# Two-layer graph attention on one core: the loads and projections ahead of the pipeline in another order, and the second layer's last eight tiles in a loop of their own

## The chip, the cores and the metric

The kernel runs on one core of one Trainium2 chip. The metric is the device time of one launch in microseconds (us); lower is better. All times below are us unless marked ns.

## The reference, cut to what matters

Sixteen graphs of 1024 nodes with 256 features each go through two layers. All arithmetic is float32; `adj` is int32 with about 3% ones.

```
# layer 0: masked 8-head attention (HD = 32), pre-norm, residual
h = relu(layernorm(x))
Q, K, V = h Wq' + bq, h Wk' + bk, h Wv' + bv
x = x + softmax(where(adj == 0, -inf, Q K' / sqrt(32))) V  Wo' + bo
# layer 1: one head, edge scores by kind of edge, pre-norm, residual
h = relu(layernorm(x))
e_k = leaky_relu((h * a_k) h', 0.2)            for k = 0..3
x = x + softmax(where(adj == k + 1, e_k, -9e15)) h
```

With the inputs at hand only kind 1 occurs. The kernel computes layer 1 for that kind and checks at the very end, in a few small instructions on `kinds_seen`, whether another kind was present; if so a slow branch is taken, which never happens here.

## The kernel before

A graph has eight tiles of 128 rows, so there are 128 tiles. Everything is laid out by hand in one `tc.manual_schedule()` block: the order in which the Python code calls the methods is the order of the instructions on each engine's queue, and each engine works its queue strictly in that order. The DMAs are issued from queues too: SP's (`nc.sync`), ACT's (`nc.scalar`) and POOL's (`nc.gpsimd`). Each DMA that SP or ACT issues takes one of eight semaphores in turn, so it also waits until the DMA that had that semaphore before it has landed.

**Classes.** `Piece` normalises rows of `x`, turns them and projects them to keys, queries and values. `piece.load` reads `x`; `stats` runs `bn_stats` and `bn_aggr` on DVE and then `norm_of`, 18 tiny POOL instructions for 1/sqrt(variance); `normed` is the scaled ReLU on ACT; `turn` transposes on PE and copies on ACT (`hT`) and DVE (`hTm`); `project(which, oc)` multiplies on PE (which = 0 keys, 1 queries; oc one of two halves of the features); `high` (ACT) and `split` (DVE) cut the result into two halves that add up to it exactly, and `split` issues the DMAs that write them to DRAM (`kd` for keys, `qd` for queries), each twice, once from SP and once from ACT when the piece has four tiles; `values` makes V. `load_key(b, h)` reads one head's keys back from `kd`, `Attend.load_queries` reads one tile's queries from `qd` (`qt`).

`Attend` is layer 0 for one tile: `scores(h)` on PE, `softmax_max(h)` on DVE (L435), `softmax_exp(h)` on ACT (L443), then the probabilities are transposed, for half the heads by PE and ACT, for the other half by a DVE 32x32 block transpose (`blocks_of`, L364) and four DMAs that put the blocks in place (`placed`, L369); `combine` multiplies with V, and later steps project, add the residual, write `x1d` and normalise for layer 1 (`turn_normed`, `turned_normed` write the tile's columns of `h1T`).

`Edges` is layer 1 for one tile: `prepare` (POOL, `ha`), `score(0)`, `score(1)` (PE, L565, into the PSUM tile `sides[1]`), `softmax_max` and `leak` (DVE, L579, L587), `softmax_exp` (ACT, L591), `turn_blocks` (DVE, L364), `place_blocks` (four SP DMAs, L369), `gather(0)`, `gather(1)` (PE, L609), `load_nodes` (POOL DMA), `store` (DVE, L618, and an SP DMA). Its buffers `sel`, `ha`, `x1b`, `pT1` exist once each.

**Prologue.** Graph 0 cannot be projected inside the loop, so it is done ahead of it in two `Piece`s of four tiles each (`first`). Then come one tile of graph 1 (`piece_was`) and the load and statistics of the next (`piece_next`). In program order: the small bias loads and the four weights are loaded and the weights are transposed; the three pieces are loaded, then normalised one after the other; adjacency tile 0 is flagged and masked, adjacency tile 1 and `piece_next` are loaded from POOL's queue, `piece_next.stats()`; then both first pieces are turned, projected (for each piece keys, then queries), and their values made; then SP loads the queries of tile 0 and the eight heads' keys.

**Loop.** `for s in range(B * NT + LAG + 1)`, that is s = 0..137. At step s the body runs attention for tile s, the tail of attention for tile s-1, layer 1 for tile s-9 (`edge`, LAG = 9) and its gather for tile s-10 (`edge_was`), and the projections of the piece for tile s+9. From s = 129 on only layer 1 is left: the last eight tiles, all of graph 15, which go through the same loop body. There the body is, in order: `score(0)`, (once) the turn of the last layer-0 tile, `turn_blocks` and `place_blocks` of the tile before, `score(1)`, `load_nodes` of the tile before, `softmax_max`, `leak`, `prepare` of the next tile, `gather(0)`, `gather(1)` and `store` of the tile before, `softmax_exp`.

Of the kernel before, what the change touches and what calls it, by code (L numbers as in the profile page):

```python
# [8 lines left out]
F32 = mybir.dt.float32  # L9
# [8 lines left out]
P = 128  # L18
HEADS = 8
# [23 lines left out]
def gnn_kernel(  # L43
# [18 lines left out]
    nc = tc.nc  # L62
# [40 lines left out]
    a_t = const.tile([P, NC, N_KINDS], F32, name="a_t")  # L103
    with nc.allow_non_contiguous_dma(reason="a few hundred elements, once"):
        nc.sync.dma_start(out=bq_t, in_=bq.rearrange("(c p) -> p c", p=P))
        nc.sync.dma_start(out=bk_t, in_=bk.rearrange("(c p) -> p c", p=P))
        for k, a in enumerate((a_0, a_1, a_2, a_3)):
            nc.sync.dma_start(out=a_t[:, :, k], in_=a.rearrange("(c p) o -> p (c o)", p=P))
    bv_t = const.tile([P, D], F32, name="bv_t")
    bo_t = const.tile([P, D], F32, name="bo_t")  # L110
    for i in range(2):
        nc.sync.dma_start(
            out=bv_t[:, i * P : (i + 1) * P].rearrange("p (r d) -> p r d", r=2),
            in_=bv.rearrange("(r i d) -> i r d", i=2, r=2)[i].partition_broadcast(P),
        )
    nc.sync.dma_start(out=bo_t, in_=bo.partition_broadcast(P))

    def transposed_weight(w, name):

        rows = work.tile([P, NC, D], F32, tag="p", name=f"{name}_rows", bufs=4)  # L120
        nc.sync.dma_start(out=rows, in_=w.rearrange("(c p) f -> p c f", p=P))
        wt = const.tile([P, NC, D], F32, name=name)
        tr = ps_tr.tile([P, 4, P], F32, tag="tr", name=f"{name}_tr")
        for fc in range(NC):
            for oc in range(NC):
                nc.tensor.transpose(tr[:, fc * NC + oc, :], rows[:, oc, fc * P : (fc + 1) * P], ident)
        if name == "wvT":
            for fc in range(NC):
                nc.vector.tensor_copy(
                    wt[:, fc].rearrange("p (i r d) -> p r i d", i=2, r=2),  # L130
                    tr[:, fc * NC : (fc + 1) * NC].rearrange("p r (i d) -> p r i d", i=2),
                )
        else:
            nc.vector.tensor_copy(wt.rearrange("p c f -> p (c f)"), tr.rearrange("p c f -> p (c f)"))
        return wt

    wqT = transposed_weight(wq, "wqT")
    wkT = transposed_weight(wk, "wkT")
    wvT = transposed_weight(wv, "wvT")
    woT = transposed_weight(wo, "woT")  # L140


    def norm_of(mv):
# [4 lines left out]
        def place(name, dtype=F32):  # L148
            return small.tile([P, 4], dtype, tag=name, name=name)[:, :n]

# [19 lines left out]

    def stats_place(n):
        return small.tile([P, 4, nc.vector.BN_AGGR_DIM], F32, tag="mv", name="mv")[:, :n, :]

# [5 lines left out]

    qds, kds, vs, keysets = {}, {}, {}, {}  # L180

    class Piece:
# [66 lines left out]
        def project(self, which, oc):  # L249
            wT, bias = ((wkT, bk_t), (wqT, bq_t))[which]  # L250
            b, w = self.b, self.n * P
# [67 lines left out]
        def values(self):  # L319
            b = self.b  # L320
            if b not in vs:
                vs[b] = graph.tile([P, NT, D], F32, tag="v", name=f"v_{b}")
            for t in range(self.n):
                ps = (late, early, brief)[t % 3]
                self.vproj = ps
                for i, hT in enumerate((self.hTm, self.hT)):
                    for fc in range(NC):
                        nc.tensor.matmul(
                            ps[:, i * P : (i + 1) * P],
                            lhsT=hT[:, fc, t * P : (t + 1) * P],  # L330
                            rhs=wvT[:, fc, i * P : (i + 1) * P],
                            start=(fc == 0),
                            stop=(fc == NC - 1),
                        )
                if self.n > 1:
                    self.biased(t)
# [41 lines left out]
    class Attend:  # L378
# [111 lines left out]
        def output(self):  # L490
            self.y = late
            for g in range(NC):
                nc.tensor.matmul(
                    self.y, lhsT=self.oT[:, g, :], rhs=woT[:, g, :], start=(g == 0), stop=(g == NC - 1)
                )
# [51 lines left out]
    class Edges:  # L547
        def __init__(self, b, t):
            self.b, self.t = b, t
            self.rows = slice(t * P, (t + 1) * P)  # L550

        def prepare(self):
            self.ha = work.tile([P, NC, P], F32, tag="ha", bufs=1)
            for c in range(NC):
# [6 lines left out]
        def score(self, nh):  # L561
            cols = slice(nh * HALF, (nh + 1) * HALF)
            self.e = sides[1]
            for c in range(NC):
# [11 lines left out]
        def softmax_max(self):  # L576
            self.sel = work.tile([P, N], F32, tag="sel", bufs=1)
            top = small.tile([P, 1], F32, tag="top")
# [16 lines left out]
        def load_nodes(self):  # L595
            self.x1 = work.tile([P, D], F32, tag="x1b", bufs=1)
            nc.gpsimd.dma_start(out=self.x1, in_=x1ds[self.b][self.rows, :])
# [4 lines left out]
        def place_blocks(self):  # L602
            self.pT = placed(self.blocks, ptp.tile([P, N], F32, tag="pT1", name="pT1", bufs=1))

# [86 lines left out]
    def edges_of(s):  # L691
        s -= LAG
        return Edges(*divmod(s, NT)) if 0 <= s < B * NT else None

# [4 lines left out]
    with tc.manual_schedule():  # L699
        first = [Piece(0, 0, 4), Piece(0, 4, 4)]  # L700
        piece_was = Piece(1, 0)
        for piece in (*first, piece_was):
            piece.load(nc.sync)
        for piece in (*first, piece_was):
            piece.stats()
            piece.normed()
        now, piece_next = attend_of(0), piece_of(0)
        nxt = attend_of(1)
        now.load()
        now.flag()  # L710
        now.mask()
        nxt.load()
        piece_next.load()
        piece_next.stats()
        for piece in first:
            piece.turn()
        for piece in first:
            for which in range(2):
                for oc in range(NC):
                    piece.project(which, oc)  # L720
                    piece.high()
                    piece.split()
        for piece in first:
            piece.values()
        piece, edge, edge_was = piece_next, None, None
        now.load_queries()
        for h in range(HEADS):
            load_key(0, h)
        piece_was.turn()
# [5 lines left out]
        gone = was = None  # L735
        for s in range(B * NT + LAG + 1):
            b, t = divmod(s, NT)
# [142 lines left out]


        seen = small.tile([P, B], F32, tag="seen", bufs=1)
        nc.vector.tensor_reduce(seen, kinds_seen.rearrange("p (b t) -> p b t", t=NT), AX.X, ALU.max)
# [48 lines left out]
```

## Time and profile before

| | |
|---|---|
| median of 3 runs | 3300.01 (3297.72 to 3308.03) |
| the profiled execution: its time, its span | 3310.77, 3309.0 |
| busy, share of the span | PE 93%, DVE 85%, ACT 74%, POOL 52% |
| mean granted TensorE clock | 0.979 |
| first softmax instruction (DVE L435) starts | 80.04 |
| last tile's store (DVE L618) starts | 3298.66 |
| layer 1 alone (s = 129 to 137) | from about 3206 to 3299 |

The profile is one execution, and its times count from the start of its span; its own time lies 1.8 over its span, and 10.8 over the median of the runs. A timeline row gives the start, the duration, the engine, the line, the instruction, out<-in, the count, and in brackets the idle time before and what ended it. "DMA share" in a table of windows is the mean busy share of the core's 16 DMA engines.

### The profile page before, as it was taken

To read this page: it belongs to the slowest core of one execution; us is meant where nothing else is said; L and a number is where in the kernel's file an instruction comes from. 1 tells how busy PE (TensorE), PEld (TensorE's weight loads), DVE (VectorE), ACT (ScalarE), POOL (GpSimd) and SP (SyncE) were. 2 spreads that over 40 slices of the span, in tenths; PEclk is the share of its full clock that TensorE was granted. 3 is DMA by queue.
4 is the path that set the end of the run, shared out by engine and by line. 5 is a ranking of instruction groups with operands and counts; after the bars stand their busy time and mean duration, and the time that the engine had idled before them with its cause. 6 is when DMAs were issued, how large, how long until landed. Compare 5 with 4: busy or idle time off the path is not lost. (4 is left out here: it accounts for less than half of the span.)

```text
span 3309.0 us, 98026 instructions
## 1 busy us (share of the span) xinstructions
PE 3080.0 (93%) x36018; PEld 2239.0 (68%) x36018; DVE 2802.7 (85%) x5111; ACT 2458.4 (74%) x4829; POOL 1735.3 (52%) x3902
## 2 busy tenths in 40 slices
PE   4888999999999999999999999999999999998997
PEld 2666767777676767767677677776766676676653
DVE  2887989989898989989899888989988899898963
ACT  2887878778787877878778777878777788787750
POOL 2555555555555555555555555555555555555531
PEclk9898999999999999999999999999999999999999
DMA  5777787877878787787878878787787877877642
GB/s 187 219 232 227 235 262 221 269 225 235 264 221 267 225 254 241 223 261 228 255 229 240 245 229 253 228 261 237 229 257 218 250 235 231 252 231 242 197 136 70
DMA packets 747063, 762.93 MB, mean 231 GB/s; under 512 B 71280, under 2 KB 692080, under 8 KB 746576
## 3 DMA queue, kind: packets, MB, share of 16 engines
q1 hardware_dynamic: 678288, 542.21, 55.3%
q0 software_dynamic: 65088, 210.16, 19.9%
q8 instruction: 290, 4.75, 0.6%
q10 hardware_dynamic: 3200, 4.19, 0.3%
q14 instruction: 197, 1.61, 0.1%
HBM read 252.98 MB, written 167.77 MB: 127 GB/s over the span
## 5 line engine op out<-in xcount | busy, mean ns | idle before, releaser
L435 DVE CUSTOM_DVE_ANT_0 p<-s,neg 128x1024 f32<-128x1024 f32 x1024 | 1233.6, 1205 | 150.6 <-issue 120.5
L443 ACT ACTIVATE p<-p,nmx 128x1024 f32<-128x1024 f32 x1024 | 1178.4, 1151 | 221.2 <-DVE nmx L435 219.7
L423 PE MATMUL s<-k,qt 128*128 128x512 f32 x2048 | 797.3, 471 | 21.8 <-DVE nmx L435 9.8
L478 PE MATMUL acc<-pT,v 128*32 128x128 f32 x16384 | 561.0, 283 | 112.3 <-DMA pT<-blocks 110.7
L544 ACT COPY pT<-trp 128x512 f32<-128x512 f32 x1024 | 543.8, 582 | 162.6 <-PE trp L543 151.9
L403 POOL TENSOR_SCALAR neg<-adj 128x1024 bf16<-128x1024 int32 x128 | 467.0, 3648 | 359.3 <-ACT neg L415 358.9
L364 DVE STREAM_TRANSPOSE blocks<-p 128x1024 f32<-128x1024 f32 x512 | 632.2, 1235 | 0.1
L478 PEld LDWEIGHTS acc<-pT,v 128*32 128x32 f32 x16384 | 472.1, 114 | 196.8 <-issue 119.4
L543 PE MATMUL trp<-ident,p 128*128 128x128 f32 x4096 | 534.2, 274 | 0.2 <-ACT pT L544 0.2
L543 PEld LDWEIGHTS trp<-ident,p 128*128 128x128 f32 x4096 | 481.0, 141 | 74.0 <-ACT pT L544 3.6
L609 PE MATMUL acc<-h,pT 128*32 128x256 f32 x8192 | 509.9, 383 | 12.5 <-DMA pT<-blocks 11.8
L565 PE MATMUL s<-h1T,ha 128*128 128x512 f32 x1024 | 482.8, 595 | 0.5 <-ACT h1T L522 0.5
L423 PEld LDWEIGHTS s<-k,qt 128*128 128x128 f32 x2048 | 331.1, 192 | 155.0 <-issue 107.7
L609 PEld LDWEIGHTS acc<-h,pT 128*32 128x32 f32 x8192 | 246.6, 110 | 228.5 <-issue 78.0
L462 POOL COPY wide<-rec 128x256 f32<-128x256 f32 x128 | 51.0, 398 | 573.3 <-DVE rec L460 573.3
L309 POOL DMA_DIRECT2D kd<-halves x240 | 169.6, 707 | 238.6 <-DVE halves L282 230.6
L579 DVE CUSTOM_DVE_ANT_0 sel<-s,neg 128x1024 f32<-128x1024 f32 x128 | 156.8, 1225 | 146.2 <-PE s L565 146.2
L565 PEld LDWEIGHTS s<-h1T,ha 128*128 128x128 f32 x1024 | 175.3, 191 | 130.0 <-issue 128.6
L591 ACT ACTIVATE sel<-sel,nmx 128x1024 f32<-128x1024 f32 x128 | 145.5, 1137 | 70.8 <-DVE rec L616 64.9
L443 ACT ACTIVATION_READ_ACCUMULATOR p<-p,nmx 128x1 f32 x1024 | 193.7, 189 | 0.0
L472 ACT COPY recT<-acc 128x256 f32<-128x256 f32 x128 | 47.8, 373 | 176.7 <-PE acc L468 176.7
L261 PEld LDWEIGHTS acc<-hT,wkT 128*128 128x128 f32 x960 | 119.5, 195 | 76.1 <-issue 46.9
(106 smaller groups left out, 4008.3 us busy)
## 6 DMA issues: line engine op xcount, KB each, us to landing
pT<-blocks SPq DMA_DIRECT2D x2560, 128.0 KB, 3.5
qt<-qd SPq DMA_DIRECT2D x128, 512.0 KB, 5.5
adj<-in_adj POOLq DMA_DIRECT2D x127, 512.0 KB, 4.8
qd<-halves SPq DMA_DIRECT2D x240, 256.0 KB, 3.2
k<-kd POOLq DMA_DIRECT2D x120, 512.0 KB, 7.0
kd<-halves SPq DMA_DIRECT2D x240, 128.0 KB, 3.8
kd<-halves POOLq DMA_DIRECT2D x240, 128.0 KB, 3.6
xb<-in_x POOLq DMA_DIRECT2D x128, 128.0 KB, 3.0
```

Source lines behind the costliest of these rows:

```text
L309: queue.dma_start(out=kds[self.b][oc, :, :, twice, self.cols], in_=halves.rearrange("p (w n) -> p w n", w=2),)
L364: nc.vector.transpose(blocks.rearrange("p b j q -> p j b q"), p)
L403: nc.gpsimd.tensor_scalar(self.neg, self.adj, 0.0, MASKED, ALU.is_equal, ALU.mult)
L423: nc.tensor.matmul(self.ps[:, cols], lhsT=self.qt[:, h, :], rhs=keysets[self.b][h][:, cols], start=True, stop=True,)
L435: nc.vector.tensor_tensor_reduce(out=p, in0=sides[h in (3, 5, 7)], in1=self.neg, scale=-SCALE, scalar=FLOOR, op0=ALU.add, op1=ALU.min, acc ...
L443: nc.scalar.activation(p, p, AF.Exp, bias=nmx, scale=-1.0, accum_out=self.sums[:, h : h + 1])
L478: nc.tensor.matmul(sums_place[r * HD : (r + 1) * HD, g * P : (g + 1) * P], lhsT=vs[self.b][:, j, place_of(h) : place_of(h) + HD], rhs=self ...
L543: nc.tensor.transpose(tr[:, j, :], p[:, jj * P : (jj + 1) * P], ident)
L544: copy(pT[:, half * 4 : half * 4 + 4, :], tr)
L565: nc.tensor.matmul(self.e[:, cols], lhsT=self.ha[:, c, :], rhs=h1Ts[self.b][:, c, cols], start=(c == 0), stop=(c == NC - 1),)
L579: nc.vector.tensor_tensor_reduce(out=self.sel, in0=self.e, in1=masks[self.b, self.t], scale=-1.0, scalar=3e38, op0=ALU.add, op1=ALU.min, a ...
L609: nc.tensor.matmul(sums_place[a * HD : (a + 1) * HD, :], lhsT=self.pT[:, j, a], rhs=h1s[self.b][:, j, :], start=(j == 0), stop=(j == NT - 1),)
```

## The change

The prologue is laid out anew. SP first loads `x` of graph 0, then the four weights (`load_weights`), then `piece_was`, adjacency tile 0, the biases (`load_biases`) and `piece_next`, which moves from POOL's queue to SP's. The statistics of the two first pieces go into one place, and one `norm_of` with eight columns serves both. The weights are transposed after that. All key projections of both pieces come ahead of all query projections, and the eight `load_key` are issued between the two. `load_queries` comes behind the query projections; flag, mask and the load of adjacency tile 1 come after them too, and `piece_next.stats()` after the values. The values of a four-tile piece use the two rotating `ps_tr` tiles of PSUM.

The loop ends after s = 128. The last eight tiles of layer 1 run in a loop of their own: tile k's scores are put ahead of the gather of tile k-2, the scores alternate between `sides[0]` and `sides[1]`, `turn_blocks` of tile k-1 stands ahead of `store` of tile k-3, and the buffers for `sel`, `pT1`, and for odd tiles `ha` and `x1b`, come from pools with free slots. The diff, cut where lines only moved into a function:

```diff
+    def load_biases():
...
+    weight_rows = {}
+
+    def load_weights():
+        for w, name in ((wk, "wkT"), (wq, "wqT"), (wv, "wvT"), (wo, "woT")):
+            weight_rows[name] = work.tile([P, NC, D], F32, tag="p", name=f"{name}_rows", bufs=4)
+            nc.sync.dma_start(out=weight_rows[name], in_=w.rearrange("(c p) f -> p c f", p=P))
...
         def place(name, dtype=F32):
-            return small.tile([P, 4], dtype, tag=name, name=name)[:, :n]
+            if n <= 4:
+                return small.tile([P, 4], dtype, tag=name, name=name)[:, :n]
+            places.append(name)
+            return many[:, len(places) * n - n : len(places) * n].bitcast(dtype)
...
-                ps = (late, early, brief)[t % 3]
+                ps = late if self.n == 1 else ps_tr.tile([P, D], F32, tag="tr", name="vproj")
...
     class Edges:
-        def __init__(self, b, t):
+        def __init__(self, b, t, last=False):
...
+            self.side = sides[t % 2 if last else 1]
+            self.tags = {"sel": ("p", 4), "pT1": ("pT", 7)} if last else {}
+            if last and t % 2:
+                self.tags |= {"ha": ("hT", 1), "x1b": ("x1", 1)}
...
         first = [Piece(0, 0, 4), Piece(0, 4, 4)]
-        piece_was = Piece(1, 0)
-        for piece in (*first, piece_was):
+        piece_was, piece_next = Piece(1, 0), piece_of(0)
+        now, nxt = attend_of(0), attend_of(1)
+        for piece in first:
             piece.load(nc.sync)
-        for piece in (*first, piece_was):
-            piece.stats()
+        load_weights()
+        piece_was.load(nc.sync)
+        now.load()
+        load_biases()
+        piece_next.load(nc.sync)
+        mv = stats_place(NT)
+        for piece in first:
+            for t in range(piece.n):
+                stats_of(piece.x[:, t, :], mv[:, piece.first + t, :])
+        r, shift = norm_of(mv)
+        for piece in first:
+            piece.norm = tuple(a[:, piece.first : piece.first + piece.n] for a in (r, shift))
             piece.normed()
-        now, piece_next = attend_of(0), piece_of(0)
-        nxt = attend_of(1)
-        now.load()
-        now.flag()
-        now.mask()
-        nxt.load()
-        piece_next.load()
-        piece_next.stats()
+        for name in ("wkT", "wqT", "wvT", "woT"):
+            weights[name] = transposed_weight(name)
+        piece_was.stats()
         for piece in first:
             piece.turn()
-        for piece in first:
-            for which in range(2):
+        for which in range(2):
+            for piece in first:
                 for oc in range(NC):
                     piece.project(which, oc)
                     piece.high()
                     piece.split()
+            if which == 0:
+                for h in range(HEADS):
+                    load_key(0, h)
+        now.load_queries()
+        piece_was.normed()
+        now.flag()
+        now.mask()
+        nxt.load()
         for piece in first:
             piece.values()
         piece, edge, edge_was = piece_next, None, None
-        now.load_queries()
-        for h in range(HEADS):
-            load_key(0, h)
+        piece.stats()
         piece_was.turn()
...
-        for s in range(B * NT + LAG + 1):
+        for s in range(B * NT + 1):
...
+        gone.turn_normed()
+        gone.turned_normed()
+        tiles = [edge_was, edge] + [edges_of(B * NT + LAG - NT + t) for t in range(1, NT)]
+        for i in range(1, len(tiles) + 2):
+            edge = tiles[i] if i < len(tiles) else None
+            if edge:
+                edge.score(0)
+                edge.score(1)
+            if i <= len(tiles):
+                tiles[i - 1].turn_blocks()
+                tiles[i - 1].place_blocks()
+            if i >= 3:
+                tiles[i - 3].store()
+            if i >= 2:
+                tiles[i - 2].load_nodes()
+            if edge:
+                edge.softmax_max()
+                edge.leak()
+                edge.softmax_exp()
+            if i + 1 < len(tiles):
+                tiles[i + 1].prepare()
+            if i >= 2:
+                tiles[i - 2].gather(0)
+                tiles[i - 2].gather(1)
+        tiles[-1].store()
```

`tiles[0]` is the last tile of graph 14, whose scores were done in step 128; `tiles[1]` to `tiles[8]` are the eight tiles of graph 15.

## The prediction

> **What bounds the kernel now.** I read the waits of the first 80 us, then the timeline there, then the DMA view, and for the end the chain that ended last. In the loop between, 128 steps of some 24, the change leaves every engine's order alone, so I look at the two ends.
>
> Waits of the first 80 us (us in total, times, longest):
>
> ```profile
> DVE st L176 <- DMA xin<-in_x: 22.8, 1, 22.8
> PE trn L231 <- DVE blocks L236: 17.9, 1, 17.9
> ```
>
> One `bn_stats` of `piece_next` stands on DVE ahead of the copies that the projections need, and waits 22.8 for its `x`. The timeline says why:
>
> ```profile
> 34.52 3.67 POOL L403 TENSOR_SCALAR neg<-adj 128x1024 bf16<-128x1024 int32 x1 [1.85 <-ACT neg L415]
> 38.49 0.79 POOL L394 DMA_DIRECT2D adj<-in_adj  x1 [0.30 <-POOL neg L403]
> 39.29 0.55 POOL L203 DMA_DIRECT2D xin<-in_x  x1
> 42.58 0.43 DVE L176 BATCH_NORM_STATS2 st<-xin 128x6 f32<-128x256 f32 x1 [22.78 <-DMA xin<-in_x]
> ...
> 46.38 5.61 PE L261 MATMUL proj<-qt,wkT 128*128 128x512 f32 x8 [0.55 <-DVE blocks L236]
> ...
> 51.69 2.73 SPq L309 DMA_DIRECT2D kd<-p  x2
> ```
>
> That load is issued by POOL behind three norms and the mask. The first projection starts at 46.38, the first key write at 51.69. Windows (span, then busy time and count of PE, PEld, DVE, ACT, POOL, granted clock, DMA share, GB/s):
>
> ```profile
> 20.00:40.00 20.00, 2.75 (x8) 1.48 (x8) 0.00 (x0) 6.83 (x13) 14.14 (x48) 1.00 0.01 1
> 60.00:80.00 20.00, 14.58 (x85) 10.42 (x84) 6.07 (x13) 3.44 (x7) 0.25 (x1) 1.00 1.07 392
> ```
>
> For 20 us nothing but POOL works; later the DMA engines are full, at 392 GB/s. So the prologue has two limits in turn: a stall on one load, then DMA.
>
> The chain that ended last, one tile of the end:
>
> ```profile
> 3258.29 1.25 DVE blocks L364
> ...
> 3261.47 2.58 DMA pT<-blocks
> ...
> 3264.09 3.65 PE acc L609 x58
> ...
> 3268.18 1.25 DVE blocks L364
> ```
>
> The period is 3268.18 - 3258.29 = 9.89: block transpose, issues and landing of four DMAs, gather, store, then the next transpose, which stands behind that store on DVE. PE does the next tile's scores while the DMAs fly and then waits for them. So the end is a chain of latencies, not an engine at work.
>
> **Prologue, step by step.** SP's first issue stays at 0.73. `x` now leads; one 512 KB load (adjacency tile 1, nothing beside it) lands 3.7 after issue, and back-to-back ones landed 1.4 apart, so I put the pieces at 4.4 and 5.8. Eight pairs of statistics at 0.53 end at 8.8. One norm of 18 POOL instructions took 17.25 to 22.41, 5.16; eight columns instead of four change little (one column cost 5.0): 14.0. Eight `normed` at 0.52 (2.07 for four) end at 18.2. ACT's first copy ends at 18.8. From DVE's first copy (43.14) to the first projection took 3.24 before, from there to the first key write 5.3; so 22.0 and 27.3, against 51.69: 24.4 earlier. The weights' transposes and four copies (3.4 on DVE) and `piece_was.stats` hide between 8.8 and 18.8, while DVE waits for POOL and ACT; uncovered they would cost at most 4. The bias loads now wait for the semaphores of earlier loads (the first for `x`) and land near 11, long before the first `high` at 26: nothing.
>
> From 27.3 the bytes rule. Sixteen writes, eight key loads and the queries of tile 0, 512 KB each, are 25 x 0.524 = 13.1 MB; at 392 GB/s that is 33.4. From first issue to first landing took 3.1, of which 1.3 is transfer, so 1.7 comes ahead: 27.3 + 1.7 + 33.4 = 62.4. Before, scores needed only the queries (77.3 by the trace's landings) and the first keys (78.6). Now the queries are last: on SP they stand behind eight key loads and four query writes. That gives back part of the 24.4. Against it stands the engines' own chain: eight projections at 2.12 to 42, eight values at 1.0 to 50, then turn and keys of `piece_was`, 3.5: 54. ACT issues its last query write only when the second key load has landed (near 45); behind it stand the flag, and then POOL's mask of 3.7 to about 50. All of it hides under 62.4; without that cover 54 would be the bound. Landing to first softmax took 1.4 (78.63 to 80.04). So 63.8 instead of 80.04: a gain of 16. Ends: 11, if the transfers pack worse, to 20, if they go at 1.25 each as the first five key loads did.
>
> The Trainium skill speaks against the rate: "DMA: Bandwidth & Descriptors", Specifications, gives a core about 358 GB/s of HBM. By it the stretch takes an estimated 36.6, and the gain is 13; the trace's 392 over 20 us is above it here.
>
> **End, step by step.** Steps up to 128 are the same. The last layer-0 tile is normalised by 3209.44, turned on PE by 3209.95. Now both score halves come behind the turn (before, `score(0)` ran at 3206.06), two more PE us here.
>
> ```profile
> 3210.38 3.22 PE L565 MATMUL s<-h1T,ha 128*128 128x512 f32 x4 [0.46 <-ACT h1T L522]
> ...
> 3277.54 3.70 PE L565 MATMUL s<-h1T,ha 128*128 128x512 f32 x8
> ```
>
> Four rows took 3.22 after a short idle, eight take 3.70 when PE is warm. PE idles longer there now (3206.1 to 3209.5). I add 1.9 for the slow start and put the first tile's scores at 3215.3.
>
> The skill ("TensorE: Matmul & The Clock Gate", What's actually happening) has half clock after an idle window of some 3.4 us and full clock after as long at work; by it the penalty could be paid a whole window longer, an estimated 1.7 more. The trace agrees in kind: the granted clock is at half for 3.4 us from 3211.0 and again from 3292.9.
>
> From there each tile costs PE one score and one gather. Back to back, start to start, that is 3.54 and 3.57 (the rows show 3.70 and 3.66 to the end of the pipeline): 7.1 per tile. Is the data there? From the end of a tile's scores: softmax_max 1.3, nmx and leak 1.4, exp 1.35: 4.05; transpose 1.25; four issues 2.5; landing 2.6; with small gaps 10.5. In PE's order two scores and two gathers lie between, 14.2. So DMAs have 3.7 to spare. The one PSUM place of the sums is freed by `store`, which stands on DVE behind the next transpose: 6.1 after a tile's scores end, and needed at 7.1; 1.0 to spare. DVE itself works 4.5 per tile. SP issues five DMAs, 3.1. POOL's `load_nodes` waits in places for a `store`, with `prepare` behind it, 3 ahead of need. So PE bounds.
>
> After the first scores come seven more and six gathers: 7 x 3.54 + 6 x 3.57 = 46.2, to 3261.5. Then gather of tile 5 to 3265.1; tile 6's waits for store 5, behind the last transpose (3261.5 + 5.9 + 0.5): 3267.5 to 3271.2; tile 7's blocks land at 3272.1; its gather takes 3.65 if PE stays warm (5.48 for its last 58 rows before, after 4.4 idle): 3275.9. Before, the last store started at 3298.66: 22 to 23 earlier. Ends: 17, if each tile takes 7.7 and the last gather runs cold, to 24. I take 22. The closing check (2 us) and what follows are unchanged.
>
> **Sum.** 16 + 22 = 38. The profiled execution's 3310.77 becomes 3273. It lay 10.8 above the median of the runs, and neither end has a reason to scale; so 3300 - 38 = 3262.
>
> **Rivals.**
>
> (a) The transfers before the first scores go slower. Under load from several queues the last three key loads landed 1.8 apart (83.6 to 89.0). At that rate the 25 take 45, the first softmax comes at 75, the gain is 5: 3273. For: three queues write and read at once now. Against: 392 GB/s was measured with SP and ACT both writing.
>
> (b) The end stays a chain of latencies: if `store`'s wait leaves no second and PE falls into step with DVE, each tile takes near 9.9 again, only the overlap at the edges is left, about 4, and 3280 results. For: only 1.0 to spare. Against: a shortfall of 1.0 lengthens a tile by what is missing, not by 2.8.
>
> (c) Nothing comes of it: the first softmax is held until 80 by a wait I have not seen, and (b) holds: 3296 to 3300.
>
> (d) Slower. The loop is entered with other offsets between SP's queue, DVE and PE; if the DMAs that place the blocks then come late in each step, every one of 128 tiles pays. It decides at 38/128 = 0.30 per tile; at 0.5 the time is 3326. For: DVE is busy 18.04 of 20 and PE 19.35 of 20 in the loop (window 3120 to 3140), so a slip is not absorbed. Against: steps mostly repeat at 23.2 to 24.5 from the tenth on, and every eighth, of about 30, lets the queues catch up.
>
> **How the numbers follow.** Forecast 0.74, (a) 0.10, (b) 0.08, (c) 0.04, (d) 0.04. The range 3250 to 3281 reaches from both ends' upper bounds (44) with a few us for the runs' own spread, through (a), to (b). A change under 0.3%, 10 us, could not be told from none. Faster by more: forecast, (a) and (b), 0.92; within it: (c), 0.04; slower: (d), 0.04.
>
> **What would show it.** Right: the 22.8 wait gone; first key write near 27, first softmax near 64 with the queries' landing just ahead; DMA near 390 GB/s from 29 to 62; at the end a period near 7.1 between gathers, PE without waits for `pT`, the last store 38 before 3298.66. Wrong: first softmax after 70 (the DMA sum), a period over 8 with PE waiting for DVE's `store` (the spare second), or a step in the loop other than 23.8 (then neither end explains it).

## The result and the profile after

The changed kernel takes 3267.22 (median of 4 runs, 3263.22 to 3271.52) beside 3301.41 of the kernel before (4 runs, 3297.72 to 3308.03): a ratio of 0.9894, 95% interval 0.9873 to 0.9916, 34 less. Run once more on another chip, as `changed_again` below, it took 3275.60 beside 3299.88: 0.9907 (0.9875 to 0.9940). The forecast was 3262, the range 3250 to 3281. The profiled execution took 3269.37 with a span of 3267.6.

The execution is best read in five pieces, each from rows of the timeline: up to the start of the first softmax instruction (DVE, L447 now); from there to the same instruction of step 127; from that to the last layer-0 tile's `residual` (DVE L511, 32 later); from the `residual` to the start of the last `store` (L640); and from that store to the end of the span.

| | before | after | less |
|---|---|---|---|
| start to first softmax | 80.04 | 67.84 | 12.2 |
| first softmax to step 127 | 3090.1 | 3081.4 | 8.7 |
| step 127 to the last `residual` | 32.5 | 32.1 | 0.5 |
| last `residual` to last `store` | 96.0 | 76.2 | 19.8 |
| last `store` to the end of the span | 10.3 | 10.1 | 0.2 |

The two ends give 32.0. The 8.7 of the second row are dealt with below: they lie within what one execution differs from another.

**The prologue.** Waits of the first 80 us: the 22.8 on `xin` is gone, and this stands in its place.

```profile
PE s L435 <- DMA qt<-qd: 14.4, 1, 14.4
```

The timeline from the first key write on:

```profile
27.53 7.02 SPq L321 DMA_DIRECT2D kd<-p  x4
...
45.71 0.37 ACTq L306 DMA_DIRECT2D qd<-p  x1
...
51.92 0.79 POOL L406 DMA_DIRECT2D adj<-in_adj  x1 [0.31 <-POOL neg L415]
...
61.28 0.36 SPq L402 DMA_DIRECT2D qt<-qd  x1
...
66.06 1.22 PE L435 MATMUL s<-k,qt 128*128 128x512 f32 x2 [14.44 <-DMA qt<-qd]
67.84 1.22 DVE L447 CUSTOM_DVE_ANT_0 p<-s,neg 128x1024 f32<-128x1024 f32 x1 [15.44 <-PE s L435]
```

The key writes begin 24.2 earlier than before (51.69). PE is ready at 66.06 - 14.44 = 51.6, and then waits for the queries, which SP issues last. The DMA view from 28 to 68, one figure per 1 us:

```profile
GB/s 84 414 401 414 404 408 410 404 414 406 410 298 231 396 368 425 407 414 401 397 411 419 412 406 410 426 375 388 390 422 386 379 388 397 305 128 345 160 2 0
```

Apart from two dips the engines move some 400 GB/s throughout. SP issues the first key read at 37.26, after 2.6 of waiting for the key writes to land, and the query read at 61.28, after two waits (4.5 in all) for query writes. Each dip, at 39 to 41 and at 62 to 64, lies some 2 behind such an issue, which fits queues that had run dry.

**The end.** The start, two tiles in the middle, the last two gathers:

```profile
3188.13 0.69 PE L530 MATMUL acc<-ident,h 128*128 128x128 f32 x2 [3.32 <-ACT h L523]
3188.61 6.22 PE L587 MATMUL s<-h1T,ha 128*128 128x512 f32 x8
3194.66 3.60 PE L587 MATMUL s<-h1T,hT 128*128 128x512 f32 x8
...
3216.55 3.70 PE L587 MATMUL s<-h1T,ha 128*128 128x512 f32 x8
...
3223.77 3.70 PE L587 MATMUL s<-h1T,hT 128*128 128x512 f32 x8
```

```profile
3247.81 5.35 PE L631 MATMUL acc<-h,pT 128*32 128x256 f32 x64 [2.31 <-DVE ot L640]
...
3253.77 3.66 PE L631 MATMUL acc<-h,pT 128*32 128x256 f32 x64 [0.61 <-DVE ot L640]
...
3257.50 0.48 DVE L640 SCALAR_TENSOR_TENSOR ot<-acc,rec,x 128x256 f32<-128x256 f32 x1 [3.71 <-PE acc L631]
```

A tile takes 3223.77 - 3216.55 = 7.22 instead of 9.89, and no gather waits for `pT`. What PE still waits for lies at the edges: 3.3 for the last layer-0 tile, after which the first scores take 6.22 instead of 3.70; 2.31 for a store, after which the last gather but one (gather 6, counting graph 15's tiles from 0) takes 5.35 instead of 3.66; and 0.61 for the next store ahead of the last gather.

### The profile page after: what moved, and what is told of

Its sections match the earlier page's. It is cut to its first block, busy times and chain, and to the rows that moved or that the text cites. A ratio compares the mean times of both kernels' runs of the same rounds, so it can differ in the third digit from the quotient of the medians.

```text
span 3267.6 us, 97986 instructions
## 1 busy us (share of the span) xinstructions
PE 3068.5 (94%) x36018; PEld 2237.6 (68%) x36018; DVE 2803.9 (86%) x5111; ACT 2453.8 (75%) x4829; POOL 1726.7 (53%) x3883
## 3 DMA queue, kind: packets, MB, share of 16 engines
q8 instruction: 290, 4.75, 0.6%
## 5 line engine op out<-in xcount | busy, mean ns | idle before, releaser
L447 DVE CUSTOM_DVE_ANT_0 p<-s,neg 128x1024 f32<-128x1024 f32 x1024 | 1233.8, 1205 | 154.2 <-issue 108.6
L435 PE MATMUL s<-k,qt 128*128 128x512 f32 x2048 | 798.0, 471 | 37.9 <-DMA qt<-qd 14.4
L376 DVE STREAM_TRANSPOSE blocks<-p 128x1024 f32<-128x1024 f32 x520 | 642.4, 1235 | 11.2 <-ACT p L613 10.8
L555 PEld LDWEIGHTS trp<-ident,p 128*128 128x128 f32 x4096 | 480.0, 141 | 72.8 <-ACT pT L556 2.7
L631 PE MATMUL acc<-h,pT 128*32 128x256 f32 x8192 | 498.8, 383 | 5.3 <-DVE ot L640 3.2
L587 PE MATMUL s<-h1T,ha 128*128 128x512 f32 x992 | 469.2, 596 | 0.0
L601 DVE CUSTOM_DVE_ANT_0 sel<-s,neg 128x1024 f32<-128x1024 f32 x120 | 147.0, 1225 | 126.6 <-PE s L587 126.6
L273 PE MATMUL acc<-hT,wkT 128*128 128x128 f32 x960 | 143.0, 294 | 24.7 <-DVE halves L294 23.5
```

Source lines behind the costliest of these rows:

```text
L273: nc.tensor.matmul(ps, lhsT=wT[:, fc, oc * P : (oc + 1) * P], rhs=(self.hT, self.hTm)[which][:, fc, :], start=(fc == 0), stop=(fc == NC - 1),)
L376: nc.vector.transpose(blocks.rearrange("p b j q -> p j b q"), p)
L435: nc.tensor.matmul(self.ps[:, cols], lhsT=self.qt[:, h, :], rhs=keysets[self.b][h][:, cols], start=True, stop=True,)
L447: nc.vector.tensor_tensor_reduce(out=p, in0=sides[h in (3, 5, 7)], in1=self.neg, scale=-SCALE, scalar=FLOOR, op0=ALU.add, op1=ALU.min, acc ...
L555: nc.tensor.transpose(tr[:, j, :], p[:, jj * P : (jj + 1) * P], ident)
L587: nc.tensor.matmul(self.e[:, cols], lhsT=self.ha[:, c, :], rhs=h1Ts[self.b][:, c, cols], start=(c == 0), stop=(c == NC - 1),)
```

## The experiments

Theory: the gain is the sum of the two ends. The first softmax is set by the bytes moved ahead of the queries; the end by PE's work, because with two tiles between scores and gather the chain of latencies no longer sets the period. The 128 steps between are untouched. Rivals: the steps became shorter because the loop is entered in another state; waits for semaphores rather than bytes hold the first scores; in the end it is the buffers, the second score place or the order on DVE that pays, not the distance.

### Each end alone

`prologue_alone` is the changed kernel with the old end:

```diff
-        for s in range(B * NT + 1):
+        for s in range(B * NT + LAG + 1):
...
-        gone.turn_normed()
-        gone.turned_normed()
-        tiles = [edge_was, edge] + [edges_of(B * NT + LAG - NT + t) for t in range(1, NT)]
...
-        tiles[-1].store()
```

> Prologue as changed, end of the loop as before. Theory (the two ends add up, the 128 steps between are untouched): first softmax at 67.8 instead of 80.0, the end again in tiles of 9.9, so 12 less than before: about 3288, ratio 0.996. Rival (the 128 steps themselves became shorter because the loop is entered with other offsets; in the profiled execution they took 8.7 less): 12 + 9 = 21 less, about 3279, ratio 0.9935, with steps 0 to 127 again about 9 shorter than in the profile before. Second rival (the head start is given back in the loop): about 3300, ratio 1.000.

3286.94 (9 runs) beside 3306.23: 0.9950 (0.9929 to 0.9970), 16 to 19 less by ratio and medians. (Here and below the ratio is the recorded one; the quotient of the two medians would be 0.9942.) First softmax 67.81; last `residual` to last `store` 94.1.

`end_alone` is the kernel before with the changed `Edges`, the loop to s = 128 and the loop for the last eight tiles:

```diff
-        for s in range(B * NT + LAG + 1):
+        for s in range(B * NT + 1):
...
+        gone.turn_normed()
+        gone.turned_normed()
+        tiles = [edge_was, edge] + [edges_of(B * NT + LAG - NT + t) for t in range(1, NT)]
...
+        tiles[-1].store()
```

> Prologue as before, the last eight tiles in their own loop. Theory: first softmax at 80, the last eight tiles 7.2 apart and PE without waits for pT, 20 less than before: about 3280, ratio 0.994; prologue alone and end alone together make up the whole gain of 34. Rival (the loop's 8.7 belong to the change): end alone gives 20 as well, but the two alone add up to some 9 more or less than the whole. Second rival (the end's gain needs the earlier prologue, by the state of the queues): under 10, ratio above 0.997.

3282.28 (6 runs) beside the same 3306.23: 0.9932 (0.9908 to 0.9956). First softmax 80.14; last `residual` to last `store` 76.6.

So each end brings its part without the other, and 0.9950 x 0.9932 = 0.9882 agrees with the 0.9894 of both. The intervals alone (some 7 to 8 either way) would not exclude the rival's 9; the profiles speak against it. From first softmax to step 127 the kernel before took 3090.1, `prologue_alone` 3076.8, `end_alone` (with the old prologue) 3080.7, the changed kernel 3081.4 and, in `changed_again`, 3089.0. Over all fourteen profiles here, with the same instructions in that stretch, it lies between 3067.1 and 3100.8, in no order that goes with the prologue: of two kernels with the changed prologue word for word, profiled on one chip one after the other, one took 3067.1 and the other 3085.9. So the 8.7 lie well within the spread of one execution against another. Which steps differ can be seen (those around a change of graph take 25 to 31, in each execution others). The granted clock in that stretch goes with it: it stood at half for some 126 us in the kernel before and 109 in the changed kernel, and half of that difference is about as much as the 8.7. It was 89 in `end_alone`, which has the old prologue, and 74 to 126 over the fourteen (correlation with the length of the stretch 0.76). No run shows whether the slower clock is the cause of the waits around a change of graph or follows from them.

### What sets the first softmax

`adjacency_early` takes one transfer out of the stretch:

```diff
+        now.flag()
+        now.mask()
+        nxt.load()
         for piece in first:
             piece.norm = tuple(a[:, piece.first : piece.first + piece.n] for a in (r, shift))
...
-        now.flag()
-        now.mask()
-        nxt.load()
```

> The changed kernel with flag and mask of adjacency tile 0 and the load of adjacency tile 1 (0.52 MB) put ahead of the normalisation, where the DMA engines idle. Theory (bytes): the queries of tile 0 land 1.3 earlier, 64.7 instead of 66.0, first softmax at 66.5. Rival (the queue runs dry before the queries are issued, and that wait sets the landing): 66.0 and 67.8 as before. Either way the time changes by less than two runs differ; the profile decides.

```profile
64.86 1.22 PE L435 MATMUL s<-k,qt 128*128 128x512 f32 x2 [13.16 <-DMA qt<-qd]
66.66 1.23 DVE L447 CUSTOM_DVE_ANT_0 p<-s,neg 128x1024 f32<-128x1024 f32 x1 [14.17 <-PE s L435]
```

Both rows are 1.2 earlier than in the changed kernel, for 0.52 MB less, which at the 400 GB/s of the DMA view is 1.3. The first softmax of the nine profiles with the unaltered prologue lies between 67.32 and 68.52, so 66.66 is outside that spread, but by 0.7 only. It speaks for bytes, although the query load is issued only after a wait (60.09 here). Its one run, 3279.79, tells nothing: that loop took 3093.2.

`first_queries_early` takes away the need for a third of the bytes:

```diff
-        for which in range(2):
-            for piece in first:
...
+        projections(first[0], 0)
+        projections(first[1], 0)
+        projections(first[0], 1)
+        for h in range(3):
+            load_key(0, h)
+        first[0].values()
+        now.load_queries()
+        load_key(0, 3)
+        projections(first[1], 1)
+        for h in range(4, HEADS):
+            load_key(0, h)
```

> The changed kernel with the order in the prologue altered: keys of both pieces, queries of the first piece, three key loads, the queries of tile 0, the fourth key load, then the queries of the second piece and four key loads. Theory (bytes ahead of the first scores set the first softmax): some 17 transfers of 0.524 MB lie ahead of the queries' landing instead of some 27; at 392 GB/s the queries land at 27.5 + 1.7 + 22.7 = 52, beside an engines' chain that was ready at 51.6: first softmax 54 to 57 instead of 67.8, and 11 to 13 less than the changed kernel: about 3255, ratio 0.986. Rival (waiting for semaphores and landings, not bytes, holds the queries): first softmax 62 or later, at most 5 less, ratio 0.988 or above. Second rival (the bytes are only moved into the first steps): first softmax near 55, but steps 0 to 7 longer by as much, total as the changed kernel's, ratio 0.9895.

```profile
55.56 1.22 PE L435 MATMUL s<-k,qt 128*128 128x512 f32 x2 [2.63 <-DMA qt<-qd]
56.94 1.23 DVE L447 CUSTOM_DVE_ANT_0 p<-s,neg 128x1024 f32<-128x1024 f32 x1 [3.22 <-POOL sq L173]
```

The first softmax comes at 56.94, 10.9 earlier, and PE waits 2.6 instead of 14.4. Step 8 starts at 226.99, where nine profiles with the changed prologue lie between 232.4 and 241.7: the first eight steps do not give it back. Time 3265.21 (5 runs) beside 3306.23: 0.9859 (0.9834 to 0.9885), the ratio of the theory, though the median lies 10 above its 3255. The runs spread from 3252.72 to 3278.14, and against the product of the two ends alone (0.9882) it is not told apart by times. The rows settle what holds the first softmax, not what a launch gains: the loop of this profile is the longest of the fourteen (3100.8), while that of `all_together`, which has early queries too, took 3082.1.

### What the end gains from

`changed_again` is the changed kernel itself, without an edit, on the chip of three others below.

> The changed kernel once more, for comparison on one chip with the next three. Every theory: about 3267 where the kernel before takes 3300, ratio 0.989 (0.987 to 0.992), with the last stores 7.2 apart; steps 0 to 127 differ from the earlier profile by up to some 10, since the same loop took 3081 to 3101 in the profiles so far.

3275.60 (6 runs, 3268.63 to 3281.23). Last `residual` to last `store` took 74.5; with the four other profiles of the same end, 74.5 to 76.6. That piece is read to 2, where whole runs are read to 10, and the rest goes by it. `one_pT1`, `store_first`, `halves_ahead` and `second_sums_place` have one run each (3279.99, 3254.41, 3270.95 and 3251.05 beside one run of the kernel before, 3286.18), whose times decide nothing.

`one_tile_apart` puts the gather of tile k-1 behind the scores of tile k:

```diff
             if i >= 2:
-                tiles[i - 2].gather(0)
-                tiles[i - 2].gather(1)
+                tiles[i - 1].gather(0)
+                tiles[i - 1].gather(1)
```

with `store` and `load_nodes` one tile closer too, and `i <= len(tiles)` as the condition.

> The changed kernel with the gather of tile k-1 behind the scores of tile k, as in the loop before, instead of the gather of tile k-2; buffers, alternating score places and the block transpose ahead of the store stay. Theory (the distance of two tiles is what takes the latency of 10.5 from scores to placed blocks off the period): PE waits for pT in every tile, two tiles take 10.5 + 3.6 + 3.6 = 17.7, a tile 8.9 (up to 9.9, if the store adds itself), so 12 to 19 more over seven tiles, 1 to 2 less at the end: 10 to 17 slower than the changed kernel, about 3277 to 3284, ratio 0.9925 to 0.9945. Rival (buffers and the second score place pay): a tile still takes 7.2, ratio 0.9894 as the changed kernel.

```profile
3216.98 3.70 PE L587 MATMUL s<-h1T,ha 128*128 128x512 f32 x8
3220.61 3.68 PE L631 MATMUL acc<-h,pT 128*32 128x256 f32 x64
3224.22 3.70 PE L587 MATMUL s<-h1T,hT 128*128 128x512 f32 x8
3228.50 0.59 PE L631 MATMUL acc<-h,pT 128*32 128x256 f32 x2 [0.58 <-DMA pT<-blocks]
...
3230.88 3.64 PE L631 MATMUL acc<-h,pT 128*32 128x256 f32 x58 [0.20 <-DMA pT<-blocks]
3234.45 3.70 PE L587 MATMUL s<-h1T,ha 128*128 128x512 f32 x8
```

Two tiles take 3234.45 - 3216.98 = 17.5 (17.7 expected). Of each two gathers one runs through (3220.61), and the other stands on the landing of its blocks again and again; a wait in every tile had been expected. The piece takes 85.9, 10 more. Time 3280.11 (9 runs) beside 3299.88: 0.9927 (0.9901 to 0.9953), where the theory had it; `changed_again`'s interval overlaps.

`one_pT1` leaves the distance and takes the buffers for `pT1` away:

```diff
-            self.tags = {"sel": ("p", 4), "pT1": ("pT", 7)} if last else {}
+            self.tags = {"sel": ("p", 4)} if last else {}
```

> The changed kernel with the single pT1 buffer of the loop before in its end. Theory (the blocks of tile k-1 can be placed only when the gather of tile k-2 is done; from there four issues, the landing and the next gather take 2.5 + 2.2 + 3.7): period 8.4 to 8.8 instead of 7.2, and the last gather 4 later: residual to last store 86 to 91. Rival (the distance of two tiles alone pays): 7.2 and 76.

```profile
3232.83 3.66 PE L631 MATMUL acc<-h,pT 128*32 128x256 f32 x64 [1.91 <-DVE ot L640]
...
3236.55 2.52 SPq L381 DMA_DIRECT2D pT<-blocks  x4
3239.11 0.61 SPq L641 DMA_DIRECT2D out<-ot  x1
3241.53 0.48 DVE L640 SCALAR_TENSOR_TENSOR ot<-acc,rec,x1b 128x256 f32<-128x256 f32 x1 [3.62 <-DMA out<-ot]
...
3242.07 3.66 PE L631 MATMUL acc<-h,pT 128*32 128x256 f32 x64 [1.94 <-DVE ot L640]
```

The piece takes 94.7: the whole gain of the end is gone, more than the 86 to 91 expected, and the period is 3242.07 - 3232.83 = 9.24, not 8.4 to 8.8. The first link was right: SP places blocks only once the gather has ended (3236.5). What I had not seen stands behind it on SP: the write of the earlier tile's output, whose landing the next store awaits, since `ot` exists once; and the next gather awaits that store. So the distance pays nothing without the buffers for `pT1`, while `one_tile_apart`, with the buffers and without the distance, keeps about half of the gain (85.9, where the kernel before took 96.0). The whole gain needs both.

`store_first` restores the order on DVE:

```diff
+            if i >= 3:
+                tiles[i - 3].store()
             if i <= len(tiles):
                 tiles[i - 1].turn_blocks()
                 tiles[i - 1].place_blocks()
-            if i >= 3:
-                tiles[i - 3].store()
```

> The changed kernel with the store of tile k-3 ahead of the block transpose of tile k-1 on DVE. Theory (that order has a spare second; PE bounds): period still 7.2, residual to last store within 1 of 76.2; only gather 6 starts some 1.7 earlier. Rival (the order of transpose and store is what keeps DVE off the path): period 7.7 or more, 79 to 80.

Period 7.22 as forecast, so the rival falls; but the piece takes 73.5, 1.0 below the lowest of the five and 2.4 below their mean of 75.8, where I had said within 1 of 76.2. The transpose ahead of the store costs nothing in the middle and something at the very end: here gather 6 waits 0.61 for its store instead of 2.31. (It takes 3.66 instead of 5.35, but so it does after 2.31 in `changed_again`.)

### What is left in the end

`halves_ahead` fills PE's idle 3.3 with score halves that need no column of the last layer-0 tile:

```diff
+        tiles[1].score(0)
+        tiles[2].score(0)
         gone.turn_normed()
         gone.turned_normed()
...
-                edge.score(0)
+                if i >= 3:
+                    edge.score(0)
```

with the second tile's `prepare` moved into step 128.

> Only the first alteration of the filled end: the first score halves of graph 15's first two tiles ahead of the last layer-0 tile's turn. Read from the residual of the last layer-0 tile to the last store, which took 74.5 to 76.6 in five profiles with the changed end and 70.5 with both alterations. Theory (idle PE time and its slow start cost 4.5 of these): 71 to 72. Rival (the store that gather 6 waits for gives most): 73.5 to 75.

`second_sums_place` gives even tiles a PSUM place of their own:

```diff
+            self.place = late if last and t % 2 == 0 else sums_place
...
-                        sums_place[a * HD : (a + 1) * HD, :], lhsT=self.pT[:, j, a], rhs=h1s[self.b][:, j, :],
+                        self.place[a * HD : (a + 1) * HD, :], lhsT=self.pT[:, j, a], rhs=h1s[self.b][:, j, :],
...
```

> Only the second alteration: the sums of even tiles in another PSUM place. Theory (the last gather is set by the landing of its blocks, 10.5 behind the last scores, so that an earlier and warmer gather 6 gains at most the 1.3 that the last gather still waited): residual to last store 75 to 76. Rival (gather 6's wait of 2.3 and its slow 1.7 are on the path in full): 72.

`end_filled` has both:

```diff
+        tiles[1].score(0)
+        tiles[2].score(0)
         gone.turn_normed()
...
+            self.place = late if last and t % 2 == 0 else sums_place
```

> The changed kernel with two alterations in its end: the first score halves of graph 15's first two tiles, which do not need the last layer-0 tile, stand ahead of that tile's turn, where PE idled 3.3; and the sums of even tiles go to a second PSUM place, so that gather 6 does not wait for a store. Theory (PE bounds the end; idle time costs itself and a slow start): the first tiles' scores are through 5.3 earlier (3.6 of work in the gap, the slow start of 2.5 gone, a wait of 0.8 for the turn left), gather 6 starts 2.3 earlier and takes 3.7 instead of 5.35, the last gather then waits for its blocks 10.5 behind the last scores: 5 to 6.6 less than the changed kernel, about 3261, ratio 0.9877. Rival (DVE or the landing of the blocks bounds the period near 7.2 as well): the 5.3 are lost to waits for pT within the tiles, the period grows to 7.5 and more, ratio 0.989.

The start of the filled end and, from `second_sums_place`, its last gathers:

```profile
3199.30 1.98 PE L588 MATMUL s<-h1T,ha 128*128 128x512 f32 x4
3201.12 1.88 PE L588 MATMUL s<-h1T,hT 128*128 128x512 f32 x4
3202.84 0.38 PE L530 MATMUL acc<-ident,h 128*128 128x128 f32 x2
3203.68 1.98 PE L588 MATMUL s<-h1T,ha 128*128 128x512 f32 x4 [0.46 <-ACT h1T L534]
```

```profile
3225.28 7.11 PE L632 MATMUL acc<-h,pT 128*32 128x256 f32 x128
...
3234.04 4.97 PE L632 MATMUL acc<-h,pT 128*32 128x256 f32 x62 [0.18 <-DMA pT<-blocks]
```

No slow start is left in the first rows (1.98 and 1.88 for a half, 0.46 of wait); in the last two rows, gathers 5 and 6 run back to back and warm, that is at the full granted clock (7.11 for both), and only the last gather still waits for its blocks. The piece takes 72.8 with the halves alone (71 to 72 expected, 73.5 to 75 by the rival), 72.6 with the second place alone, 70.5 with both, against 75.8 on average. So the two are worth about 3 each, and 5.3 together (5 to 6.6 expected), each from one profile, where profiles of the same end lie up to 2.1 apart. For the second place I had said 75 to 76: that was wrong, and the rival, which put gather 6's wait and slowness on the path in full, was nearly right (72). In the changed kernel the last gather waits 0.61 for a store, not for its blocks, which had landed at 3252.4; so gather 6 and the stores around it were the path. In the other four profiles of this end gather 6 ran at full clock, and yet the last gather started 11.4 to 12.1 behind the last scores, where it is 11.9 in the changed kernel. From `changed_again`:

```profile
3257.39 7.73 SPq L641 DMA_DIRECT2D out<-ot  x3
3259.80 0.48 DVE L640 SCALAR_TENSOR_TENSOR ot<-acc,rec,x1b 128x256 f32<-128x256 f32 x1 [4.98 <-DMA out<-ot]
...
3260.34 3.66 PE L631 MATMUL acc<-h,pT 128*32 128x256 f32 x64 [1.87 <-DVE ot L640]
```

It is the wait of `one_pT1` once more: `ot` exists once, SP issues the write of tile 5's output only behind the four placements of tile 7, the store of tile 6 waits for that write to land, and the last gather for that store (1.87 to 2.50 in the four). A second `ot`, or another queue for the write, was not tried. In time `end_filled` is 3273.85 (6 runs) beside 3299.88, 0.9898 (0.9866 to 0.9930), where 3261 and 0.9877 had been expected: below `changed_again` by less than the runs can tell.

### All of it

`all_together` joins the early queries, the early adjacency load and the filled end, puts the second piece's query projections behind `piece_was`, and moves the closing check's reductions into the last loop:

```diff
+        for h in range(2):
+            load_key(0, h)
+        first[0].values()
+        now.load_queries()
+        for h in range(2, 4):
+            load_key(0, h)
...
+        piece_was.turned()
+        projections(first[1], 1)
...
+            if i == 4:
+                seen = small.tile([P, B], F32, tag="seen", bufs=1)
+                nc.vector.tensor_reduce(seen, kinds_seen.rearrange("p (b t) -> p b t", t=NT), AX.X, ALU.max)
```

> The changed kernel with the first piece's queries and the queries of tile 0 early (two key loads ahead of them), the second piece's query projections behind the keys of the graph 1 tile, adjacency tile 1 loaded in the idle stretch, the end filled as above, and the closing check's reductions moved into the last loop. Theory (all of it adds up): first softmax at 53 to 55 (13 to 15 less than 67.8), the end 5 to 6.6 shorter, the closing check 1.8: 20 to 23 less than the changed kernel, about 3245, ratio 0.983. Rival (step 0 pays for the second piece's queries and the later key loads): first softmax near 54 but step 8 starts only 8 to 10 earlier than with the changed kernel, total 12 to 16 less, ratio 0.985.

3256.50 (6 runs, 3247.30 to 3263.11) beside 3299.88: 0.9856 (0.9825 to 0.9888). All its runs lie below all of `changed_again`'s on the same chip; the medians are 19.1 apart (20 to 23 expected, 12 to 16 by the rival; the 3245 expected in time was missed by 11). By the pieces it should be 23: first softmax at 53.97 (13.9 less than 67.84), last `residual` to last `store` 69.8 (6.4 less than 76.2), 7.1 instead of 10.1 from there on. Step 8 starts at 220.65, 12 to 21 ahead of the nine profiles above, so the head start holds that far. No version has a lower ratio, but that of `first_queries_early` (0.9859) is the same within the intervals.

## Why the prediction was right, point by point

**Prologue, up to the bytes: right.** Pieces of `x` at 4.67 and 6.02 (4.4 and 5.8 predicted), norm done at 14.4 (14.0), `normed` at 18.45 (18.2), first projection at 22.21 (22.0), first key write at 27.53 (27.3), ACT's last query write at 45.71 (near 45), PE ready at 51.6 (54).

**"25 x 0.524 = 13.1 MB ... 62.4": the term that was too small.** The queries landed at 66.0. From 29.2, where the bytes begin, that is 36.8 instead of 33.4. I had left out adjacency tile 1, issued by POOL at 51.92 in the middle of the stretch, and two transfers of 128 KB for the next pieces: 377 GB/s from 29 to 66 is 13.95 MB, 0.9 more than 13.1, or 2.2 at 392. `adjacency_early` shows one of these transfers at 1.2. The two dips of the DMA view fall short of 410 GB/s by 291 and 387 GB/s in slices of 1 us, some 1.7 in all; I had counted no time in which the queues run dry. The full slices were a little faster than 392, which gives some of it back.

The Trainium skill's per-core HBM figure ("DMA: Bandwidth & Descriptors", Specifications) gave an estimated 36.6 for the stretch and a gain of 13. Its result is nearer than mine (36.8 and 12.2 were measured), but not by its reason: 28 of the 35 slices from 28 to 63 stand at 386 GB/s or more, above that figure, and it was bytes and dips that made the difference.

**"Landing to first softmax took 1.4": 1.8.** From the first score to the softmax took 67.84 - 66.06 = 1.78; in `first_queries_early` it took 1.38. The clock is not what sets them apart: it was granted at 0.50 around the first scores of both (66.0 to 67.9 here, 55.5 to 57 there), and their row is 1.22 long in both. Where the 0.4 come from stays open. The gain was 12.2 instead of 16, near the lower of its two ends (11).

**The end: mechanism right, three small terms short.** PE bounds, no gather waits for `pT`, and the store's spare second is there: period 7.22 (7.1 predicted), about 0.7 over six tiles. The rows give 3.63 from a score's start to the gather's (3230.99 to 3234.62) and 3.59 from there to the next score (3238.21), where I had 3.54 and 3.57. From the last layer-0 tile's norm to the end of the first scores took 6.7 (5.9): the slow start cost 2.5, not 1.9. That size is partly luck: the same first scores took 4.74, 4.73 and 4.75 in `end_alone`, `first_queries_early` and `changed_again`, and 3.60, with no slow start, in `adjacency_early`. The last gathers: from the end of the last scores (3241.9) to the last store 15.6 (14.4). I had started the last gather at the landing of its blocks, 10.6 behind the last scores; it started 11.9 behind them, after the store of tile 6, a wait that the sum leaves out. Gather 6's half clock, which I had warm, is little of it: in `changed_again`, where it ran warm, the last gather started 11.4 behind, and the stretch took 15.2. Together 2.7, and 19.8 instead of 22. Here the Trainium skill ("TensorE: Matmul & The Clock Gate", What's actually happening) and the trace part: it puts the fall to half clock after an idle window of some 3.4 us; 2.31 were enough here and 2.06 in `one_tile_apart`, while 3.35 in `adjacency_early` were not followed by it.

**The loop: nothing that can be told, as predicted.** The profile after seems to say 8.7; fourteen profiles say that one execution cannot.

**Sum.** 38 predicted, 32.0 by the pieces, 34 and 24 by the medians of the two comparisons; that the 34, and with it the 3267 beside 3262, came so near is in part the spread of the runs. Two slips of the working changed little: 25 transfers at 1.25 take 31.3, so the upper end of the prologue's gain is 18, not 20; and 3261.5 + 5.9 + 0.5 is 3267.9, not 3267.5 (gather 6 did start 5.9 behind the last scores). **Rivals.** (a) transfers went at 36.8 / 27, 1.4 each, not 1.8. (b) did not happen, but `one_tile_apart` and `one_pT1` show that it was one tile of distance or one buffer away: 10 and 18.5 more. (c) and (d) fell with the first row that moved and with the loop.

## What to carry to other kernels

Count every transfer that any queue issues into a stretch that is bound by bytes, POOL's too, and then ask which of the bytes the first consumer needs: the changed kernel moved all of graph 0's queries before tile 0's. A chain of latencies is broken by distance and by buffers together, and a single buffer behind the same queue can undo all of it. When runs differ by ten and a change is worth five, cut the timeline at fixed instructions and compare the pieces.

## What had not been expected of the hardware

PE's clock fell after a shorter wait than I had reckoned with, and not each time. Windows of the changed kernel around gather 6 (span, then busy time and count of PE, PEld, DVE, ACT, POOL, granted clock, DMA share, GB/s):

```profile
3248.00:3250.00 2.00, 2.00 (x28) 1.11 (x24) 0.00 (x0) 0.00 (x0) 0.54 (x1) 0.62 0.66 160
3250.00:3252.00 2.00, 2.00 (x24) 0.99 (x20) 0.00 (x0) 0.00 (x0) 0.00 (x0) 0.52 0.69 211
```

2.31 of waiting, then half clock for some 3.4 (a share of 0.76 of the first window and 0.96 of the second), and a gather of 5.35. `halves_ahead` has the same after 2.30. But the same gather after the same wait, in `end_alone`:

```profile
3257.95 3.66 PE L619 MATMUL acc<-h,pT 128*32 128x256 f32 x64 [2.31 <-DVE ot L628]
```

There the granted clock stayed at 1.00, and so it did after 2.31 in `first_queries_early`, `adjacency_early` and `changed_again`. In `one_tile_apart` 2.06 were enough for the last gather (6.75 at 0.75), and 2.92 ahead of the first scores were not (1.00). So in these runs the length of the wait alone does not decide; what else does was not tried. At the start of the end, after 3.3, the half clock lasted longer in the changed kernel: 0.58 from 3188 to 3195, which is 5.9 of the 7; in `adjacency_early`, after 3.35, the clock stayed at 1.00.

The other surprise is the loop: the same instructions, from 3067.1 to 3100.8 over fourteen executions, and 19 apart on one chip. The time at half clock explains a part of it at most: with half of that time taken off, the stretch still takes from 3018 to 3043.
